# Attention's PSUM in two rings of banks, and bias products over the whole array

## The chip, the cores and the metric

The kernel runs on one NeuronCore of a Trainium2 chip. The metric is the time on the device in microseconds (us), of the one core, as the median of several executions. Engines are called by the names that the profile uses: PE is TensorE (matmuls), PEld its loading of stationary operands, DVE is VectorE, ACT is ScalarE, POOL is GpSimd, SP is SyncE, which here issues most DMA transfers.

## The reference

The input x has 32 sequences of 256 tokens with 128 features, so 8192 tokens. Four layers follow one another; each is

```python
x = x + attn(layernorm(x))
x = x + ffn(layernorm(x))
```

with these bodies:

- Layer 0: a projection to u, v and g of 256 features each; u goes through a depthwise convolution of three taps and silu, then through a diagonal state recurrence (64 states per feature); `y * sigmoid(g) + silu(v)` is projected back with a bias. The ffn has 16 experts of which each takes its best tokens, and a shared expert.
- Layer 1: linear attention with a gate and a causal mask (no softmax); the ffn has 8 experts of 512 hidden features with GELU, two per token, weighted, each `gelu(x @ w1 + b1) @ w2 + b2`, and a shared expert with biases.
- Layer 2: causal softmax attention with 16 heads of 8 features, low-rank projections; the ffn is a linear layer with a shared and six routed low-rank parts.
- Layer 3: a linear layer, a recurrence along the tokens, a second linear layer with bias `b_out`; the ffn is softmax attention over all keys of a sequence (16 heads of 8, biases), layernorms, and 8 experts (`relu(x @ w1 + b1) @ w2 + b2`, 256 hidden features), one per token.

For every softmax attention what has to come out is `softmax(q k^T / sqrt(8)) v`, then a product with `wo`.

## The kernel before, in words

Tokens lie as 64 tiles of 128 (partitions) by 128 features in the core's memory; four tiles make a block. The stages run one after another, and each opens its own pools of PSUM banks. By the time line: layer 0's mixer until about 330 us, its ffn until 750, layer 1 until 1310 and its experts until 1640, layer 2's attention from 1685 to 2240, layer 2's ffn and layer 3's mixer (function `middle`) until 2440, layer 3's attention until 3083, its experts until 3240, the rest until the end.

**Biases by matmul.** A bias row in f32 is split by `split` (L96) into three bf16 rows that add up to it. It is added to a PSUM tile by a matmul of these 3 rows with 3 rows of ones, as the first or last member of an accumulation. In layer 0's `project` (L757 to L774) the rows are 12 (`brow`, three for each of the four rows of `cwr`) and the other operand is `inside`, which says which tokens see which case. There are 128 of those, one after each six f32 matmuls over the whole 128 by 128 array; each such product is one quarter of a PSUM tile. The other places are layer 0's output (L872, 16 times), layer 1's values (L1463, 16), layer 1's output with the shared expert's bias (L1568, 16), `leave` in `middle` (L2280, 16) and the experts.

**Experts** (`Slots.experts`, L484). Tokens sorted by expert are gathered in groups of N = 2 tiles of 128. In `fetch` (L502) SP's DMA brings the group's rows `xs`, VectorE copies the expert's weights `w` (L515) and second bias `b2` (L517), PE transposes the rows (L522), VectorE copies them to `xT` (L524). `rise` (L527) makes the hidden features (L533) and ScalarE applies the activation (L539). `fall` (L544) makes the output: for each of two tiles the FC products (L549) and then the three-row bias (L553); VectorE multiplies by the token's weight (L555), and GpSimd sends both tiles to their places in DRAM (L479). The order for PE, ACT, DVE and SP is written by hand: rise(g), fetch(g+1), fall(g-1). Layer 1 has 72 groups with FC = 4, layer 3 has 40 with FC = 2.

**Attention** (L1603 to L1987), for layers 2 and 3. An item is one sequence; it takes four steps g = 0 to 3, each with four head pairs' worth of work (p, j). The order for PE, ACT and DVE is written by hand in `step` (L1921). For each of the four, two score products are made: `highs` (L1785) gives q by k, of which VectorE takes the row maximum in `maxima` (L1799, reduce at L1803); this runs LEAD = 7 steps ahead of the other, `weights` (L1842), which gives k by q with the maximum subtracted (it comes in through rows of q, the `row` below), and ScalarE makes the exponential `e` from it (L1857). In layer 2 `cover` (L1702) adds the mask by bf16 matmuls to both. `values` (L1860) of the step before multiplies `e` with the values, 16 small matmuls into the bank `o`; after g = 3 ScalarE copies `o` out.

Around these stand whole-array parts, once per item: `turn` (L1728) transposes the next input; `project` (L1739, matmul L1743) makes q and k, of which ScalarE copies the high part and VectorE (`lows`, L1754) the low part, and SP carries all to `qs` and `keys` through DRAM; `contents` (L1773) makes the values; `halve` (L1809) turns the maxima into a high and a low half on VectorE, `lower` (L1820) transposes them on PE, and its `place` has VectorE copy them to `row` and SP write them into `qs` (four DMAs); `heads` (L1883) transposes the output back on PE and VectorE divides by the sums (L1893, L1894); `back` (L1896) transposes again; `join` (L1904) is the product with `wo`, and its `add` has VectorE add it to x.

The work appended to the list `late` (`lows`, `place`, `add`) is emptied by `settle`, which runs after the first maximum of the next step. The step's order is: four times scores and maximum, with `settle` after the first; at g1 `heads`, at g2 `back`; `values`; at g0 `project` and `halve`; at g1 `lower` and `turn`, in one bank; at g3 `join` and `contents`, in one bank.

**PSUM.** [...] attention's pools are (L1714 to L1717) `ps` with 3 for `highs`, `pt` with 3 for `weights`, `pa` with 1 for `values`, and `pm` with 1, given out by `bank` (L1725), for all the whole-array parts. A tile from a pool waits until the tile that had the bank before is used up. `more` lets a caller place its own work at the end of a step: in layer 3 this is `gate` (L2412), which takes a tile from `bank` to transpose outputs and make the router's logits for the experts.

## Time and profile before

| | |
|---|---|
| median of 3 runs | 3316.81 us (3314.72 to 3318.75) |
| profiled execution, its own time | 3323.56 us |
| its span, first to last instruction | 3321.8 us |
| granted TensorE clock, mean | 0.89 |
| PE busy | 2661.6 us, 80% of the span |
| DVE busy | 1843.3 us, 55% |
| ACT busy | 1409.0 us, 42% |
| POOL busy | 844.5 us, 25% |
| largest group on DVE | L1803, the maxima: 1024 of 616 ns, 598.6 us |
| largest group on ACT | L1857, the exponentials: 1024 of 546 ns, 493.7 us |

The profiled execution is one run, recorded instruction by instruction. A group's line gives how often it ran, its busy time, the mean duration of one, and how long its engine stood idle just before its instructions, with what released them. A time line gives each instruction's start and duration. Matmuls overlap, so the distance between two starts is what one costs, not its duration. A step of attention is measured from the first L1849 of one step to that of the next.

### The profile page before, as it was taken

How to read it: one execution, taken by the hardware profiler on the slowest of the kernel's cores; microseconds unless marked ns; L12 is line 12 of the kernel's file. 1: busy time of each engine (PE TensorE's matmuls, PEld its weight loads, DVE VectorE, ACT ScalarE, POOL GpSimd, SP SyncE). 2: the span in 40 equal slices, each digit the busy share in tenths (PEclk: the TensorE clock that was granted, in tenths of full speed). 3: DMA queues.
4: the chain of work that ended last, by engine and by line, in shares of the span. 5: the costliest groups of instructions: out<-in, count | busy, mean ns of one | idle time of the engine just before them, and what ended most of it. 6: DMA issues, size and time to landing. Idle time of an engine off the chain costs nothing.

```text
span 3321.8 us, 59216 instructions
## 1 busy us (share of the span) xinstructions
PE 2661.6 (80%) x21597; PEld 1897.2 (57%) x21598; DVE 1843.3 (55%) x5368; ACT 1409.0 (42%) x2988; POOL 844.5 (25%) x1227
## 2 busy tenths in 40 slices
PE   5999778999795457999778998988988888786580
PEld 4765444446564335888656777757655555554460
DVE  6115445436874111333368877755788877774446
ACT  3323432223463222333425555557246655553123
POOL 0001444300015341444310010001501332323463
PEclk9899889999898778999869999997979988997795
DMA  2377455620002010122165444420054444440223
GB/s 67 110 247 238 177 233 228 232 73 6 11 1 88 26 35 15 60 62 61 55 180 152 131 138 141 131 64 1 8 147 119 116 115 115 122 115 13 83 80 107
DMA packets 263262, 340.80 MB, mean 103 GB/s; under 512 B 34598, under 2 KB 231062, under 8 KB 254780
## 3 DMA queue, kind: packets, MB, share of 16 engines
q1 hardware_dynamic: 231228, 237.01, 25.1%
q0 software_dynamic: 27584, 97.92, 7.7%
q8 instruction: 171, 2.80, 0.4%
q10 hardware_dynamic: 4160, 2.10, 0.2%
q14 instruction: 119, 0.97, 0.1%
HBM read 156.72 MB, written 177.83 MB: 101 GB/s over the span
## 4 chain that ended last, share of the span: by engine, by line
PE 36%; DVE 16%; issue 5%; another core or an unknown queue 5%; ACT 4%; DMA 3%; POOL 2%; SPq 1%; DVEq 0%; POOLq 0%; ACTq 0%
DVE top L1803 6%; PE hp L533 5%; PE o L549 5%; PE t L1849 4%; PE o L1870 4%; PE s L1791 2%; DMA q<-row 2%; PE o L1568 2%; POOL f_back L479 1%; ACT e L1857 1%; DVE st_x L241 1%; PE hp L1554 1%; PE m L1743 1%; PE m L1908 1%
## 5 line engine op out<-in xcount | busy, mean ns | idle before, releaser
L1803 DVE TENSOR_REDUCE top<-s 128x3 f32<-128x384 f32 (+1 forms) x1024 | 598.6, 616 | 212.9 <-PE s L1702 111.2
L1857 ACT ACTIVATE e<-t 128x384 f32<-128x384 f32 (+1 forms) x1024 | 493.7, 546 | 140.0 <-PE s L1702 76.6
L1849 PE MATMUL t<-q,k 64*128 64x256 f32 (+1 forms) x2048 | 422.9, 313 | 103.0 <-ACT e L1857 77.9
L1791 PE MATMUL s<-k,q 48*128 48x256 f32 (+1 forms) x2048 | 446.5, 333 | 12.7 <-DVE top L1803 10.1
L1849 PEld LDWEIGHTS t<-q,k 64*128 64x128 f32 x2048 | 303.4, 195 | 185.4 <-ACT e L1857 108.9
L1791 PEld LDWEIGHTS s<-k,q 48*128 48x128 f32 x2048 | 312.9, 201 | 27.4 <-DVE top L1803 20.0
L479 POOL DMA_INDIRECT f_back<-y,place x224 | 216.3, 965 | 313.1 <-DVE y L555 171.8
L539 ACT ACTIVATE h<-hp,w 128x256 f32<-128x256 f32 x368 | 154.6, 471 | 328.6 <-PE hp L533 287.2
L1870 PE MATMUL o<-e,val 128*32 128x256 f32 (+1 forms) x4096 | 270.2, 385 | 0.0
L549 PE MATMUL o<-w,h 128*128 128x128 f32 x1472 | 214.3, 284 | 0.0
L533 PE MATMUL hp<-xT,w 128*128 128x256 f32 x736 | 195.2, 405 | 21.2 <-DVE xT L524 15.6
L549 PEld LDWEIGHTS o<-w,h 128*128 128x128 f32 x1472 | 183.5, 193 | 7.7
L2039 POOL TENSOR_SCALAR xn<-x_sb,mean_x,r_x 128x128 f32<-128x128 f32 x64 | 53.0, 836 | 441.7 <-PE m L1732 387.2
L1870 PEld LDWEIGHTS o<-e,val 128*32 128x32 f32 x4096 | 112.0, 114 | 91.9 <-issue 38.8
L533 PEld LDWEIGHTS hp<-xT,w 128*128 128x128 f32 x736 | 134.2, 195 | 46.2 <-DVE xT L524 20.2
L1554 PE MATMUL hp<-xnT,shared 128*128 128x512 f32 x128 | 74.2, 709 | 103.4 <-ACT h L1558 93.2
L1702 PE MATMUL s<-hideq,pick 64*128 64x128 bf16 x1024 | 151.5, 231 | 0.0
L473 POOL DMA_INDIRECT f_rows<-row,slot x128 | 122.9, 960 | 110.3 <-ACT h L1558 66.9
L1702 PE MATMUL t<-hidek,pick 64*128 64x128 bf16 x1024 | 146.2, 226 | 0.0
L555 DVE TENSOR_TENSOR y<-o,xs 128x256 f32<-128x256 f32 x112 | 47.4, 424 | 164.4 <-PE o L553 149.2
L766 PE MATMUL up<-wc,hT 128*128 128x128 f32 x768 | 129.2, 309 | 0.0
L1574 DVE TENSOR_TENSOR x_sb<-x_sb,o 128x512 f32<-128x512 f32 x16 | 11.0, 687 | 209.9 <-remote 98.9
(515 smaller groups left out, 5392.8 us busy)
## 6 DMA issues: line engine op xcount, KB each, us to landing
f_rows<-blank POOLq DMA_DIRECT2D x176, 390.0 KB
tz<-kpad SPq DMA_DIRECT2D x64, 512.0 KB
d<-high SPq DMA_DIRECT2D x128, 256.0 KB
d<-low SPq DMA_DIRECT2D x128, 256.0 KB
q<-d SPq DMA_DIRECT2D x128, 256.0 KB
k<-d SPq DMA_DIRECT2D x128, 256.0 KB
xs<-f_rows SPq DMA_DIRECT2D x112, 130.0 KB
t<-f_back SPq DMA_DIRECT2D x24, 512.0 KB
```

Source lines behind the costliest of these rows:

```text
L473: i = self.K.nc.gpsimd.indirect_dma_start(self.rows, bass.IndirectOffsetOnAxis(ap=slot, axis=0), row, None)
L479: i = self.K.nc.gpsimd.indirect_dma_start(self.back, bass.IndirectOffsetOnAxis(ap=place, axis=0), row, None)
L533: nc.tensor.matmul(hp[:, i, :], w[:, (c + i) * P : (c + i + 1) * P], xT, start=True, stop=True,)
L539: nc.scalar.activation(h[:, c + i, :], hp[:, i, :], act, bias=w[:, b1 : b1 + 1])
L549: nc.tensor.matmul(o[:, i, :], h[:, c, i * P : (i + 1) * P], w[:, F + c * D : F + c * D + D], start=c == 0, stop=False,)
L766: nc.tensor.matmul(o, hT[:, 2 * blk + b, s : s + P], wc[:, j, cs], start=j == 0, stop=False)
L1702: nc.tensor.matmul(t.rearrange("p (n q) -> p n q", n=3)[:, 0:3:2, 64 * n : 64 * n + 64], pick[r, n, :], hide[name][r], start=False, stop=n ...
L1791: nc.tensor.matmul(s[:, lo:hi], q[r, p, h * P : (h + 1) * P], k[r, p, 0 : hi - lo], start=h == 0, stop=not causal and h == 1,)
L1803: nc.vector.tensor_reduce(tops[b][:, :, j, p], out_of["s"][:, 0:used].rearrange("q (h k) -> q h k", h=3 if causal else 2), axis=AX.X, op=A ...
L1849: nc.tensor.matmul(t[:, kh * SEQ : kh * SEQ + SEQ - skip], k[r, p, kh * P : (kh + 1) * P], q[r, p, skip:SEQ], start=kh == 0, stop=not caus ...
L1857: nc.scalar.activation(e, t, AF.Exp)
L1870: nc.tensor.matmul(o[32 * i : 32 * i + 32, skip:SEQ], val[b % RING][:, kh, 4 * m + i, 16 * s : 16 * s + 32], e[:, kh * SEQ : kh * SEQ + SE ...
```

## The change

It has two parts.

First, every operand of a bias matmul has 128 rows in place of 3 or 12. `split` returns a tile of 128 partitions that GpSimd has set to zero, with the rows written into its head; the ones, `inside` and the copies of `b2` have 128 partitions likewise. In `fall` one bias matmul, with `b2` repeated for both tiles, opens the accumulation of the whole bank, where two had closed it.

Second, attention's PSUM is given out as two rings. `pm` is gone. `ps`, whose tiles VectorE empties, has 4 banks in layer 2 (causal) and 3 in layer 3, and serves `highs`, `project`, `lower`, `heads`, `join` and `gate`. `pt`, whose tiles ScalarE empties, has 3 in layer 2 and 4 in layer 3 and serves `weights`, `turn`, `contents` and `back`. `values` comes ahead of all whole-array parts; `lower` stands right behind `halve` at g0 in place of g1, and the tile that it shared with `turn`, and that which `join` shared with `contents`, are two tiles each. The division in `heads` and VectorE's part of `gate` go on `late`; `more` is called ahead of the last `settle`.

```diff
@@ -95,9 +95,13 @@
         nc = self.nc
-        shape = list(t.shape)
-        hi, mid, out = (pool.tile(shape, BF16, name=f"{n}_{name}") for n in ("hi", "mid", "rows"))
+        n, *shape = t.shape
+        hi, mid = (pool.tile([n, *shape], BF16, name=f"{i}_{name}") for i in ("hi", "mid"))
+        full = pool.tile([P, *shape], BF16, name=f"rows_{name}")
+        nc.gpsimd.memset(full, 0.0)
+        out = full[0:n]
         nc.vector.tensor_copy(hi, t)
@@ -105,7 +109,7 @@
         nc.vector.scalar_tensor_tensor(out, hi, m[:, 0:1], out, ALU.mult, ALU.add)
-        return out
+        return full
@@ -513,8 +517,8 @@
                 nc.vector.tensor_copy(w, flat[:, bass.ds(at, REST)])
-                b2 = gp.tile([3, D], BF16, name="b2")
-                nc.vector.tensor_copy(b2, flat[0:3, REST:][:, bass.ds(at, D)])
+                b2 = gp.tile([P, D], BF16, name="b2")
+                nc.vector.tensor_copy(b2, flat[:, REST:][:, bass.ds(at, D)])
                 place = gp.tile([P, N], mybir.dt.uint32, name="place")
@@ -544,13 +548,16 @@
                 o = po.tile([P, N, D], F32, name="o")
+                nc.tensor.matmul(
+                    o, self.every, b2.unsqueeze(1).to_broadcast([P, N, D]), start=True, stop=False
+                )
                 for i in range(N):
                             o[:, i, :], h[:, c, i * P : (i + 1) * P],
-                            w[:, F + c * D : F + c * D + D], start=c == 0, stop=False,
+                            w[:, F + c * D : F + c * D + D], start=False,
+                            stop=i == N - 1 and c == FC - 1,
                         )
-                    nc.tensor.matmul(o[:, i, :], self.every[0:3, :], b2, start=False, stop=True)
                 y = gp.tile([P, N, D], F32, name="y")
@@ -723,13 +730,14 @@
         brow = K.split(sp, cwr, part, "brow")
-        inside = sp.tile([R, SEQ], BF16, name="inside")
-        nc.vector.tensor_copy(inside, valid)
+        inside = sp.tile([P, SEQ], BF16, name="inside")
+        nc.gpsimd.memset(inside, 0.0)
+        nc.vector.tensor_copy(inside[0:R], valid)
         half_g = sp.tile([P, 2], F32, name="half_g")
         obias = K.split(sp, out_b, K.parts(sp, 3), "obias")
-        ones3 = sp.tile([3, P], BF16, name="ones3")
-        nc.gpsimd.memset(ones3, 1.0)
+        every = sp.tile([P, P], BF16, name="every")
+        nc.gpsimd.memset(every, 1.0)
...
@@ -1286,11 +1294,10 @@
             K.second_biases(bp, b2, "f1_b2")
-            bv = sp.tile([3, D], BF16, name="bv")
+            bv = sp.tile([P, D], BF16, name="bv")
             nc.vector.tensor_copy(
             )
-        three = S.every[0:3, :]
@@ -1461,7 +1468,7 @@
                 nc.tensor.matmul(
-                    vp, three, bv.unsqueeze(1).to_broadcast([3, 4, D]), start=True, stop=False
+                    vp, S.every, bv.unsqueeze(1).to_broadcast([P, 4, D]), start=True, stop=False
                 )
...
@@ -1583,7 +1591,7 @@
                 assert not (active or ready or turned)
-                nc.scalar.copy(w_all[0:3, :, 2 * F + FC :], b2[:, 0:NE, :])
+                nc.scalar.copy(w_all[:, :, 2 * F + FC :], b2[:, 0:NE, :])
                 S.finish(rw, LONG, expert, start)
@@ -1711,10 +1719,10 @@
     dp = K.pool(es, tag + "d", 3, DRAM)
-    ps = K.pool(es, tag + "ps", 3, PSUM)
-    pt = K.pool(es, tag + "pt", 3, PSUM)
+    ps = K.pool(es, tag + "ps", 4 if causal else 3, PSUM)
+    pt = K.pool(es, tag + "pt", 3 if causal else 4, PSUM)
     pa = K.pool(es, tag + "pa", 1, PSUM)
-    pm = K.pool(es, tag + "pm", 1, PSUM)
     x_of, xT_of, tops, exps, out_of, on_of, oT_of = {}, {}, {}, {}, {}, {}, {}
@@ -1723,11 +1731,12 @@
     def bank():
-        return pm.tile([P, 512], F32, name="m")
-    def turn(b, t):
+        return ps.tile([P, 512], F32, name="s")
+    def turn(b):
         x = x_of.pop(b)
+        t = pt.tile([P, 512], F32, name="t")[:, 0:SEQ]
         for h in range(2):
@@ -1770,9 +1779,10 @@
-    def contents(b, t):
+    def contents(b):
         xT = xT_of.pop(b)
+        t = pt.tile([P, 512], F32, name="t")[:, 0:SEQ].rearrange("p (h d) -> p h d", h=2)
         for h in range(2):
@@ -1785,7 +1795,7 @@
         q, k = qs[b % RING], keys[b % RING]
-        s = out_of["s"] = ps.tile([P, 512], F32, name="s")
+        s = out_of["s"] = bank()
         r = slice(64 * j, 64 * j + TOP)
@@ -1817,10 +1827,10 @@
-    def lower(b, t):
+    def lower(b):
         cut = tops.pop(b)
-        t = t[0 : 2 * HEADS].rearrange("n (h q) -> n h q", h=2)
+        t = bank()[0 : 2 * HEADS, 0:SEQ].rearrange("n (h q) -> n h q", h=2)
         for h in range(2):
@@ -1843,7 +1853,7 @@
         r = slice(64 * j, 64 * j + 64)
-        t = pt.tile([P, used], F32, name="t")
+        t = pt.tile([P, 512], F32, name="t")[:, 0:used]
         for kh in range(2):
@@ -1888,22 +1898,29 @@
         t = t.rearrange("p h m (n c) -> p (h m n) c", c=16)
-        rec = wp.tile([P, 2 * HEADS], F32, name="rec")
-        on = on_of[b] = wp.tile([P, 2 * HEADS, HD], F32, name="on")
-        nc.vector.reciprocal(rec, t[:, :, ONE])
-        nc.vector.tensor_mul(on, t[:, :, 0:HD], rec.unsqueeze(2).to_broadcast([P, 2 * HEADS, HD]))
+        def divide():
+            rec = wp.tile([P, 2 * HEADS], F32, name="rec")
+            on = on_of[b] = wp.tile([P, 2 * HEADS, HD], F32, name="on")
+            nc.vector.reciprocal(rec, t[:, :, ONE])
+            nc.vector.tensor_mul(
+                on, t[:, :, 0:HD], rec.unsqueeze(2).to_broadcast([P, 2 * HEADS, HD])
+            )
+        late.append(divide)
         on = on_of.pop(b).rearrange("p (h n) c -> p h (n c)", h=2)
-        t = bank()[:, 0:SEQ]
+        t = pt.tile([P, 512], F32, name="t")[:, 0:SEQ]
         for h in range(2):
-    def join(b, t):
+    def join(b):
         oT = oT_of.pop(b)
+        t = bank()[:, 0:SEQ].rearrange("p (h d) -> p h d", h=2)
         for h in range(2):
@@ -1941,50 +1958,43 @@
                 beside()
-        if g == 1 and gone:
-            heads(before)
-        if g == 2 and gone:
-            back(before)
         if 0 <= t - 1 < total:
             halve(known)
+            lower(known)
         if g == 0 and then:
             x_of[ahead + 1] = rows(ahead + 1)
-        if g == 1:
-            known = a // TURNS - 1
-            if then or 0 <= known < NB:
-                m = bank()
-                if 0 <= known < NB:
-                    lower(known, m[:, SEQ:])
-                if then:
-                    turn(ahead + 1, m[:, 0:SEQ])
-        if g == 3 and (gone or fetch):
-            m = bank().rearrange("p (n h d) -> p n h d", n=2, h=2)
-            if gone:
-                join(before, m[:, 0])
-            if fetch:
-                contents(ahead, m[:, 1])
+        if g == 1 and gone:
+            heads(before)
+        if g == 1 and then:
+            turn(ahead + 1)
+        if g == 2 and gone:
+            back(before)
+        if g == 3 and gone:
+            join(before)
+        if g == 3 and fetch:
+            contents(ahead)
         beside()
+        more(t, bank, late)
         if t >= total:
             settle()
-        more(t, bank)
         for b in range(FIRST):
-            turn(b, bank()[:, 0:SEQ])
+            turn(b)
             project(b)
             settle()
-            contents(b, bank()[:, 0:SEQ].rearrange("p (h d) -> p h d", h=2))
+            contents(b)
         x_of[FIRST] = rows(FIRST)
         settle()
-        more(None, bank)
+        more(None, bank, late)
...
@@ -2318,7 +2328,7 @@
         y = row[:, :, 0:D]
-        b2 = sp.tile([3, NE, D], BF16, name="b2")
+        b2 = sp.tile([P, NE, D], BF16, name="b2")
         expert = sp.tile([1, S.groups], mybir.dt.int32, name="expert")
@@ -2409,7 +2419,7 @@
-            def gate(bank):
+            def gate(bank, late):
@@ -2431,19 +2441,23 @@
                     turned.append((new, yT))
-                if old:
-                    lo, at = old[0] // CHUNK * CHUNK, old[0] % CHUNK
-                    if at == 0:
-                        logits[lo] = lw.tile([P, CHUNK, NG + NE], F32, name="lge")
-                    nc.vector.tensor_add(
-                        logits[lo][:, at : at + 2, :], out,
-                        gate_b.unsqueeze(1).to_broadcast([P, 2, NG + NE]),
-                    )
-                    if at == CHUNK - 2:
-                        active.append((choose(lo), lo))
-                for g in count:
-                    hold[g[1]] = t[:, 384:512]
-                    go(g)
+                def then():
+                    if old:
+                        lo, at = old[0] // CHUNK * CHUNK, old[0] % CHUNK
+                        if at == 0:
+                            logits[lo] = lw.tile([P, CHUNK, NG + NE], F32, name="lge")
+                        nc.vector.tensor_add(
+                            logits[lo][:, at : at + 2, :], out,
+                            gate_b.unsqueeze(1).to_broadcast([P, 2, NG + NE]),
+                        )
+                        if at == CHUNK - 2:
+                            active.append((choose(lo), lo))
+                    for g in count:
+                        hold[g[1]] = t[:, 384:512]
+                        go(g)
+                late.append(then)
@@ -2539,16 +2553,18 @@
-            def more(t, bank):
+            def more(t, bank, late):
                     while active or pairs or turned:
-                        gate(bank)
+                        gate(bank, late)
+                        while late:
+                            late.pop(0)()
                         for g in list(active):
                 if t % TURNS == 2 or t >= NB * TURNS:
-                    gate(bank)
+                    gate(bank, late)
...
```

The hunks left out are the same edits as those at L1461 in layer 0's output, layer 1's output and `leave`, the three operands' new shapes there, and the new argument of `more` in layer 2.

## The prediction

> **What bounds the kernel now.** I read the page's first part (busy time by engine) and fourth part (the chain), then busy time by stage, then the instructions of one expert group and of one attention item.
>
> ```profile
> PE 2661.6 (80%) x21597; PEld 1897.2 (57%) x21598; DVE 1843.3 (55%) x5368; ACT 1409.0 (42%) x2988; POOL 844.5 (25%) x1227
> PE 36%; DVE 16%; issue 5%; another core or an unknown queue 5%; ACT 4%; DMA 3%; POOL 2%; SPq 1%; DVEq 0%; POOLq 0%; ACTq 0%
> ```
>
> TensorE sets the end where its order is not broken by a wait. By stage (us, then busy PE, weight loads, VectorE, ScalarE, GpSimd, clock, DMA share, GB/s), layer 1's experts, then layer 2's attention, then layer 3's:
>
> ```profile
> 1310.00:1640.00 330.00, 324.72 (x2016) 277.50 (x2016) 125.77 (x365) 122.14 (x290) 139.40 (x151) 0.98 0.20 58
> 1685.00:2240.00 555.00, 496.10 (x6837) 381.65 (x6836) 411.22 (x1254) 297.03 (x702) 48.22 (x77) 0.94 0.47 132
> 2441.00:3083.00 642.00, 507.42 (x4916) 330.36 (x4917) 471.15 (x1377) 370.78 (x793) 166.38 (x216) 0.88 0.36 103
> ```
>
> The experts are PE alone (98%). In layer 2 VectorE (74%) has slack, in layer 3 PE is idle for 21%. Who causes the idle time is in the groups of TensorE, first for 1745 to 2155 us (layer 2), then for 2500 to 2990 (layer 3); after the bar are busy us and mean ns, then idle us and releasers:
>
> ```profile
> L1849 PE MATMUL t<-q,k 64*128 64x256 f32 x404 | 150.2, 373 | 8.2 <-DMA q<-row 7.3 <-ACT val L1780 0.5
> L1825 PE MATMUL m<-ident,cut 128*32 128x128 f32 x50 | 9.7, 275 | 21.9 <-DVE on L1894 9.9 <-DVE v_x L268 6.3 <-DVE r_x L277 1.3
> ```
>
> ```profile
> L1849 PE MATMUL t<-q,k 64*128 64x256 f32 x816 | 161.8, 320 | 67.9 <-ACT e L1857 58.5 <-issue 9.1
> L1825 PE MATMUL m<-ident,cut 128*32 128x128 f32 x52 | 10.3, 280 | 18.1 <-DVE on L1894 6.7 <-DVE m L2475 3.5 <-DVE t_x L289 2.5
> ```
>
> The one `m` bank makes `lower` wait for `heads`' multiply (L1894), 22 and 18 us; in layer 3 the three `t` banks make weights wait for the exponential, 58 us.
>
> [...] the timeline of PE in one fall (start, duration) shows:
>
> ```profile
> 1434.31 1.06 PE L549 MATMUL o<-w,h 128*128 128x128 f32 x8
> 1435.30 0.22 PE L553 MATMUL o<-b,every 3*128 3x128 bf16 x1
> 1435.45 1.16 PE L549 MATMUL o<-w,h 128*128 128x128 f32 x8
> ```
>
> [...] one that waits for a bank holds all behind it, as the idle before L1825 shows. [...] the pools used 3+3+1+1 of them, so the four banks of a ring are found by giving up `m`.
>
> **The bias edits.** From the single instructions: pitch of L549's matmuls 0.112 us; previous matmul to bias 0.207 (+0.095); bias to next 0.154; that one's follower comes at 0.214 instead of 0.112 (+0.10). One three-row bias costs 0.095+0.154+0.10 = 0.35; a group has two, 0.70. A whole-array bf16 product is visible elsewhere:
>
> ```profile
> 1010.31 0.22 PE L398 MATMUL u<-taken,first 128*128 128x128 bf16 x1 [1.30 <-DVE lg L1349]
> 1010.37 0.22 PE L399 MATMUL u<-taken,every 128*128 128x128 bf16 x1
> 1010.42 0.55 PE L1509 MATMUL o<-v,a 128*128 128x129 f32 x3
> ```
>
> Pitch 0.055 for 128 columns, then f32 follows with some 0.055 extra and no drain. The new bias has 256 columns: 0.11+0.055 = 0.165, or 0.215 if the switch of type costs more. Saved per group 0.49 to 0.54. In layer 1 (72 groups, period 4.44, PE busy throughout) that is 35 to 39: **−37**. GpSimd's two sends (2.5 us) and ScalarE (1.9) stay under 3.9; gathered rows land 4.45 us after their issue with some 5.05 left to them, so they stay hidden.
>
> In layer 3 (40 groups) the period is set by those rows instead: two groups per some 6.5 us, which is place to y two groups later 1.53, 0.45, landing 4.5. A fall shorter by 0.5 shortens a pair by up to 0.5: 20 pairs, 0 to 10, taken **−9**.
>
> In layer 0's projection the 12-row bias follows every six matmuls, 128 times, at 0.352 each by the same three gaps (0.73 in cold stretches). With 128 columns the new one is 0.11 to 0.165: 0.19 to 0.24 saved, ×128 = 24 to 31 if PE sets all. The second half of it has PE busy 90 of 90 us, but DMA share 0.70, 0.74 at the shorter time; the first half waits in some blocks for VectorE's layernorm. I take **−20** (−10 to −28). 64 more (L872, L1463, L1568, leave) stand mostly in waits: **−4**. The new memsets (six in `split`, one for `inside`) are GpSimd's, in stages' openings beside loads: 0 to +2, taken 0. The wider copies of b2 have the same length per partition: 0. Sum: −37−9−20−4 = **−70** (−50 to −85).
>
> **The attention edits.** Per item (four steps g0 to g3) the steps start, by L1849, at these medians apart: layer 2: 3.68, 4.7, 2.98, 3.8 = typically 15.7, mean 16.07; layer 3: 3.81, 5.6, 3.84, 3.87 = 17.1. All my time inside a step is from its first score.
>
> Gains. [...] The wait before L1825 goes too (21.9 us over the window's 25 items, 0.88 each), and layer 3's wait for the exponential at g1 (58.5 us over 26 items, 2.3 each).
>
> Costs. Every whole-array tile that VectorE empties (project's by `lows`, lower's by the copy to `row`, heads' by `divide`, join's by add, all of them after the next step's first maximum) now sits in a ring with the scores. A score waits for the tile four back (three in layer 3), and everything behind it on PE waits too, the weights' products and so ScalarE's exponentials. VectorE, from DVE's timeline in layer 2 around g1:
>
> ```profile
> 1969.41 0.17 DVE L1812 TENSOR_TENSOR top<-top 128x16 f32<-128x16 f32 x1
> 1969.93 0.18 DVE L1818 TENSOR_TENSOR cut<-top,high 128x32 f32<-128x32 f32 x1
> 1970.26 0.56 DVE L1803 TENSOR_REDUCE top<-s 128x3 f32<-128x384 f32 x1
> 1970.73 0.75 DVE L1758 TENSOR_TENSOR low<-m,high 128x256 fp32r<-128x256 f32 x2
> 1971.39 1.48 DVE L1803 TENSOR_REDUCE top<-s 128x3 f32<-128x384 f32 x3
> ```
>
> The first maximum ends at 0.66+0.47 = 1.13 after the step's start, the two `lows` at about 1.88, `row` behind them at 2.2, `divide` (0.35+0.42 with gaps) at 1.98, add (0.41) at 1.58. Natural score starts in layer 2: 0, 0.38, 0.80, 1.28, phase 1.83.
>
> Layer 2, ring of four. g0: the fourth score waits for add (1.28 to 1.58: +0.30); `lower`, now behind project, waits for halve (0.7 us of VectorE after the last maximum): +0.3 to 0.5, and its own 0.22; 3.68 becomes 4.6 to 4.8. g1: the third score is four behind project's tile: waits for `lows` to 1.9 instead of 0.80: stall 1.13, score phase 1.83+1.13, values 0.79, heads and turn 0.80: 4.55 against 4.7. g2: fourth score waits for `divide`, 1.28 to 1.98: 2.98+0.71 = 3.70. g3: 3.71 against 3.8. Sum 16.6 to 16.7 against 15.7 to 16.07: +0.6 to +1.0, times 32 items = 19 to 32, **+25**. `place` is issued earlier, but its four row transfers stand on SP behind d<-high, d<-low, q<-d and k<-d, 11.4 to 12 us from g1 to landing, so it brings the rows no sooner; the wait for q<-row (7.3 us) stays.
>
> Layer 3, ring of three, natural scores at 0, 0.34, 0.58, 0.82, end 1.04. g0: third waits for add (1.63), scores end 2.12; `lower` waits for halve, 4.4 to 4.7: 4.92 against 3.81. g1: second waits for `lows` (2.07), third for `row` (2.4), end 2.82: 4.83 against 5.6, where the exponential's wait had been. g2: third waits for `divide` (2.02), end 2.46: 4.60 against 3.84. g3: third waits for the gate's add (1.33): 4.1 against 3.87. Sum 18.45 against 17.1: +1.35, times 32 = 43; a stretch of items 20 to 26 loses time to GpSimd's sends whatever PE does, so **+36** (0 to +47).
>
> **Sum.** −70+25+36 = −9: the profile's own 3323.6 us becomes 3314.6. The median is 6.8 less, 3316.8−9 = **3308**.
>
> **The rivals.**
> - Waits only move, because VectorE has 26% spare and its order lets the ring run ahead: attention comes out even. For it: the 22, 18 and 58 us of idle that go. Against: the first maximum stands ahead of `lows`, `divide` and add in VectorE's order. −70: 3247.
> - Slower: project's tile in VectorE's ring. In g1 the score that needs its bank waits for `lows`, and the stall is passed to the exponentials, values and the next step's maxima. The price has to pass 70 us, 1.1 us per item over 64 items, to decide; at 1.5 (my 1.35 of layer 3 in both layers, and a little for later rows) it is +95: 3342. [...] Against: layer 2 has a fourth bank.
> - Attention gains: a fourth `t` bank ends the 58 us of waits, and L1825's 40 go[...] minus small new waits: −40 beside −70: 3207.
> - The bias edit doesn't do what it says: the gaps are of bf16 beside f32, not of three rows. Then only having one product in place of two helps: 72×0.35 = 25, little more elsewhere, about −28; with +61: 3350. Against: the L398 to L1509 pitch.
>
> **How the numbers follow.** My forecast, net −30 to +12: 0.37 (range 3287 to 3329). Even attention 0.25; slower 0.25; attention gains 0.06; bias ineffective 0.07. The 8-in-10 range leaves out attention's gain, and the upper ends of the last two: 3238 (even attention, bias at −79) to 3360. A measurement of this kernel tells 0.2%, 6.6 us. Faster: even and gaining (0.31) and half of mine (0.19) = 0.50; same: a third of mine, 0.12; slower: a sixth of mine with the two slower cases, 0.38.
>
> **What would show it.** Right: an expert group of 3.9 us in layer 1 with one bias of 0.165 and no 0.207 gap; in g1 an idle before L1791 put down to DVE `low` (L1758 or L1760), in g2 to `on`, in g0 L1825 released by `cut`; in layer 3 no wait of L1849 for `e`; items of 16.6 and 18.4 us. Wrong: if L1791's idle stays under 0.3 us per item, attention is even or gains; if the group stays above 4.2, the row count was not the drain; if experts of layer 1 show PE waiting for xs, the rows were not hidden.

## The result, and the profile after

The changed kernel takes **3294.29 us** (median of 5, 3284.55 to 3301.19) against 3316.81: ratio 0.9927, 95% interval 0.9904 to 0.9949. The forecast was 3308, 9 us less than before; it became 22.5 less. The profiled execution took 3286.0 us with a span of 3284.3, so it is one of the shorter of the five, 37.5 below that of before.

Where the time went, by stage, from the first and last instructions of the stages in the two profiled executions (us):

| stage | before | after | difference | in the forecast |
|---|---|---|---|---|
| layer 0's mixer, from the first projection | 327.0 | 295.6 | −31.4 | −20 and part of −4 |
| layer 1's shared expert | 286.0 | 275.6 | −10.4 | part of −4 |
| layer 1's experts | 332.3 | 288.0 | −44.3 | −37 |
| layer 2's attention | 545.6 | 579.3 | **+33.7** | +25 |
| layer 3's attention | 641.3 | 670.0 | **+28.7** | +36 |
| layer 3's experts | 181.4 | 174.6 | −6.8 | −9 |
| all else | 1008.2 | 1001.2 | −7.0 | 0 |

The bias part gave more than forecast and attention lost what was forecast, +62 against +61. But in layer 2 most of the loss is not made of the waits that the forecast lists. First the parts that went as written: TensorE's timeline in layer 1's experts (start, duration) after the change:

```profile
1292.31 1.24 PE L537 MATMUL hp<-xT,w 128*128 128x256 f32 x5
1293.39 0.38 PE L526 MATMUL t<-ident,xs 128*128 128x128 f32 x2
1293.61 0.27 PE L551 MATMUL o<-b,every 128*128 128x256 bf16 x1
1293.72 1.95 PE L556 MATMUL o<-w,h 128*128 128x128 f32 x16
1295.50 0.38 PE L537 MATMUL hp<-xT,w 128*128 128x256 f32 x1
```

One bias product, 0.11 us to the next start (it lasts 0.27; the two overlap) and no gap ahead of it, where the forecast had 0.165 to 0.215. The sixteen matmuls of `fall` (two are recorded for each f32 product) run through. The group takes 3.85 us in place of 4.44, 0.59 less. In layer 0's projection it is 0.06 in place of 0.154:

```profile
171.25 0.94 PE L774 MATMUL up<-wc,hT 128*128 128x128 f32 x6
172.02 0.22 PE L777 MATMUL up<-rows_brow,inside 128*128 128x128 bf16 x1
172.08 0.33 PE L774 MATMUL up<-wc,hT 128*128 128x128 f32 x1
```

Then attention. Busy time, clock and DMA of its two stages after (columns as in the prediction):

```profile
1598.00:2177.00 579.00, 528.43 (x6826) 398.29 (x6827) 405.04 (x1226) 302.13 (x697) 48.08 (x67) 0.89 0.44 124
2358.00:3028.00 670.00, 554.45 (x4951) 364.70 (x4951) 477.74 (x1354) 390.47 (x792) 160.56 (x211) 0.88 0.36 103
```

The same products as before (6826 for 6837 recorded) keep TensorE busy 528 us in layer 2 in place of 496, and the granted clock is 0.89 in place of 0.94. Idle time did not grow, as the groups of TensorE from 1655 to 2095 us (layer 2) show:

```profile
L1859 PE MATMUL t<-q,k 64*128 64x256 f32 x411 | 154.9, 379 | 7.1 <-ACT val L1790 5.5 <-issue 0.8 <-DMA q<-row 0.6
L1835 PE MATMUL s<-ident,cut 128*32 128x128 f32 x52 | 10.3, 280 | 22.6 <-DVE cut L1828 10.7 <-DVE dif_x L261 4.7 <-DVE r_x L299 4.4
```

`lower` waits as long as before (22.6 us for 21.9), now for `halve`; the wait for the rows is gone (0.6 for 7.3). From 2450 to 2960 us (layer 3):

```profile
L1859 PE MATMUL t<-q,k 64*128 64x256 f32 x793 | 184.1, 326 | 0.0
L1801 PE MATMUL s<-k,q 48*128 48x256 f32 x793 | 172.8, 335 | 74.3 <-DVE top L1813 67.1 <-DVE low L1769 3.8 <-issue 1.0
```

The weights' wait for the exponential (67.9 us of idle before) is zero; the scores stand idle 74.3 us in its place, for VectorE. Before, from 2500 to 2990 us, it was 0.6:

```profile
L1791 PE MATMUL s<-k,q 48*128 48x256 f32 x816 | 160.9, 320 | 0.6 <-DVE top L1803 0.4 <-issue 0.2
```

That is the trade that the two rings make in layer 3.

What took the time in layer 2 shows when each item (0 to 31) is taken alone. Items 19 to 22 (the item's window, then the columns as above):

```profile
1953.21:1969.30 16.09, 14.72 (x215) 11.34 (x215) 10.92 (x28) 9.83 (x23) 1.57 (x2) 1.00 0.46 135
1969.30:1984.69 15.39, 14.67 (x215) 11.35 (x216) 10.92 (x28) 9.08 (x21) 1.57 (x2) 1.00 0.49 141
1984.69:2001.85 17.16, 16.17 (x215) 12.15 (x214) 12.75 (x44) 9.46 (x22) 1.57 (x2) 0.90 0.44 125
2001.85:2019.01 17.16, 16.16 (x215) 12.11 (x215) 11.25 (x31) 9.46 (x22) 1.57 (x2) 0.90 0.45 128
```

The same 215 matmuls take 14.7 us of TensorE at clock 1.00 and 16.2 at 0.90. Inside the third of these items, at the end of g0, in slices of 0.68 us:

```profile
1987.66:1988.34 0.68, 0.68 (x4) 0.35 (x2) 0.68 (x2) 0.37 (x1) 0.00 (x0) 1.00 0.00 0
1988.34:1989.02 0.68, 0.10 (x1) 0.00 (x0) 0.58 (x5) 0.55 (x2) 0.00 (x0) 1.00 0.00 0
1989.02:1989.70 0.68, 0.39 (x4) 0.21 (x4) 0.39 (x4) 0.10 (x1) 0.00 (x0) 1.00 0.00 0
```

And in two stretches of 3.41 us, the second of which is the one at half clock:

```profile
1988.58:1992.00 3.42, 2.57 (x34) 2.05 (x34) 2.48 (x11) 1.87 (x5) 0.00 (x0) 1.00 0.46 153
1992.00:1995.41 3.41, 3.41 (x29) 2.08 (x27) 1.61 (x7) 0.78 (x3) 0.17 (x1) 0.50 0.72 204
```

TensorE is idle for 0.87 us ahead of `lower` at the end of g0; 2.7 us after that, and after the score stall at the start of g1, the clock is halved for 3.4 us, and g1 takes 5.45 us in place of 4.08. Of items 8 to 28 of layer 2, 9 stand below a clock of 0.95; before the change it was one. In the 3.42 us ahead of this drop TensorE counts as busy for 2.57.

In all 13 traces every change of the clock lies on one grid of 3.413 us, to within 4 ns (1.4 in that of the result). So it matters where an item falls on that grid. An item that is hit takes some 17 us, about five periods (17.07), so the next one falls on nearly the same place and is hit too: items 21 to 28 follow one another.

### The profile page after: what moved, and what is told of

It reads as the page before. It is cut to its first block, busy times and chain, and to the rows that moved or that the text cites. A ratio compares the mean times of both kernels' runs of the same rounds, so it can differ in the third digit from the quotient of the medians.

```text
span 3284.3 us, 59072 instructions
## 1 busy us (share of the span) xinstructions
PE 2612.5 (80%) x21486; PEld 1904.8 (58%) x21486; DVE 1844.3 (56%) x5368; ACT 1434.8 (44%) x2988; POOL 851.7 (26%) x1234
## 4 chain that ended last, share of the span: by engine, by line
PE 36%; DVE 18%; another core or an unknown queue 5%; issue 5%; POOL 3%; ACT 2%; DMA 1%; SPq 1%; DVEq 0%; ACTq 0%; POOLq 0%
DVE top L1813 7%; PE o L1880 6%; PE t L1859 4%; PE hp L537 4%; PE o L556 4%; PE s L1801 3%; POOL f_back L483 2%; DVE st_x L245 2%; PE o L1576 1%; PE s L1899 1%; PE s L1925 1%; PE hp L1561 1%; PE s L1710 1%; PE t L1710 1%
## 5 line engine op out<-in xcount | busy, mean ns | idle before, releaser
L1867 ACT ACTIVATE e<-t 128x384 f32<-128x384 f32 (+1 forms) x1024 | 511.9, 543 | 188.6 <-PE s L1710 93.9
L1801 PE MATMUL s<-k,q 48*128 48x256 f32 (+1 forms) x2048 | 466.7, 343 | 110.4 <-DVE top L1813 81.8
L1859 PE MATMUL t<-q,k 64*128 64x256 f32 (+1 forms) x2048 | 465.2, 321 | 15.4 <-ACT val L1790 5.5
L1859 PEld LDWEIGHTS t<-q,k 64*128 64x128 f32 x2048 | 325.5, 200 | 65.2 <-issue 33.4
L1880 PE MATMUL o<-e,val 128*32 128x256 f32 (+1 forms) x4096 | 284.6, 401 | 0.0
L537 PE MATMUL hp<-xT,w 128*128 128x256 f32 x736 | 186.2, 393 | 30.5 <-DVE xT L528 17.7
L556 PE MATMUL o<-w,h 128*128 128x128 f32 x1472 | 185.2, 278 | 0.0
L556 PEld LDWEIGHTS o<-w,h 128*128 128x128 f32 x1472 | 175.9, 194 | 1.6
L1561 PE MATMUL hp<-xnT,shared 128*128 128x512 f32 x128 | 74.3, 713 | 105.4 <-ACT h L1565 101.2
L336 POOL DMA_DIRECT2D f_rows<-blank x176 | 98.3, 558 | 54.5 <-POOL blank L332 51.5
```

Source lines behind the costliest of these rows:

```text
L537: nc.tensor.matmul(hp[:, i, :], w[:, (c + i) * P : (c + i + 1) * P], xT, start=True, stop=True,)
L556: nc.tensor.matmul(o[:, i, :], h[:, c, i * P : (i + 1) * P], w[:, F + c * D : F + c * D + D], start=False, stop=i == N - 1 and c == FC - 1,)
L1561: nc.tensor.matmul(hp, shared[:, c * P : (c + 1) * P], xnT[:, blk, :], start=True, stop=True)
L1801: nc.tensor.matmul(s[:, lo:hi], q[r, p, h * P : (h + 1) * P], k[r, p, 0 : hi - lo], start=h == 0, stop=not causal and h == 1,)
L1859: nc.tensor.matmul(t[:, kh * SEQ : kh * SEQ + SEQ - skip], k[r, p, kh * P : (kh + 1) * P], q[r, p, skip:SEQ], start=kh == 0, stop=not caus ...
L1867: nc.scalar.activation(e, t, AF.Exp)
```

## The experiments

The kernels were timed in five sittings: in two of them (the result; e5 to e8) the kernel before took 3317 to 3319 us, in the other three (e1 to e4; e9 and e10; e11) 3146 to 3156; these are called the first and the second place. So ratios to before in the same sitting are compared, and stages only within one place or where they agree. Items are counted from 8 to 28 of each layer, "low" below a clock of 0.95.

**The two parts alone.** e1 takes the bias edits without those of attention and `gate`, e2 the others.

```diff
 e1:
-        three = sp.tile([3, P], BF16, name="three")
+        every = sp.tile([P, P], BF16, name="every")
...
 e2:
-    pm = K.pool(es, tag + "pm", 1, PSUM)
+    ps = K.pool(es, tag + "ps", 4 if causal else 3, PSUM)
+    pt = K.pool(es, tag + "pt", 3 if causal else 4, PSUM)
...
```

> The kernel before with the bias edits alone; attention, its banks and gate as before. My theory (the two parts add up, and the bias part gives what the stages outside attention gained, about -98 us): 3219 us, layer 2's attention 545 us from its first score to its last join and layer 3's 654, as before. Rival (the bias part is worth my -70 and the rest of the gain came with the attention part, by the clock or by shifted transfers): 3247. Rival (attention's loss comes from the bias edits too): attention's stages 579 and 683, time 3290.

> The kernel before with the attention edits alone (two rings, order, late parts), biases with 3 and 12 rows. My theory: +62 us, 3379; layer 2's attention 579 us with steps g0 4.65 in undisturbed items, layer 3's 683. Rival (waits only move): 3317, stages 545 and 654. Rival (attention gains and something else lost it): 3277.

Measured: e1 3060.99 us, **0.9732** (0.9706 to 0.9758), layer 2's attention 543.7 us as before. e2 3207.83 us, **1.0219** (1.0179 to 1.0258). The product is 0.9945, and the changed kernel has 0.9927: the parts add up, attention is a loss on its own, and the rival of moving waits only falls. Scaled to the first place that is −89 and +73 us.

By stage, layer 2's attention takes 543.7 us in e1 and 555.8 in e2, layer 3's 596.2 and 629.5. The 579 that was expected for layer 2 in e2 is missed: only 1 of its 21 items is low, against 9 in the changed kernel's trace with the same attention. So the new order costs +12 us in layer 2 with hardly a drop of the clock, and +33 in layer 3, where 14 of 21 items are low and 6 in e1. The traced execution of e2 was the shortest of its four (3191.0 us to 3227.9).

**Rows or number of products.** e3 keeps one opening product per group but gives it three rows.

```diff
-    o, self.every, b2.unsqueeze(1).to_broadcast([P, N, D]), start=True, stop=False
+    o, self.every[0:3, :], b2[0:3].unsqueeze(1).to_broadcast([3, N, D]),
+    start=True, stop=False,
```

> As the bias edits alone, but the experts' one opening bias product has 3 rows in place of 128 (256 columns as there). It tells the drain from the number of products. If the drain of the short product is the cost: a group of layer 1's experts takes 0.24 to 0.35 us more than the 3.85 with 128 rows, about 4.1 to 4.2, and the experts' stage of layer 1 some 17 to 25 us more. If it was only that two products became one: 3.85, no difference.

Measured: one time, 3085.68 us. From the first to the last product of `fall` in layer 1 it takes 293.8 us against 273.1 of e1, +20.7, or 0.29 per group (in nine other kernels with 128 rows it is 272.8 to 273.2). TensorE's timeline, to be read against the one above (its line L557 is L556 there):

```profile
1199.19 0.38 PE L526 MATMUL t<-ident,xs 128*128 128x128 f32 x2
1199.51 0.28 PE L551 MATMUL o<-b,every 3*128 3x256 bf16 x1
1199.71 2.05 PE L557 MATMUL o<-w,h 128*128 128x128 f32 x16
```

The gap ahead grows from 0.22 to 0.32 after the pair of transposes, the one behind from 0.11 to 0.20, and the sixteen matmuls take 2.05 in place of 1.95. So the number of rows is what costs, in the same three places as before, and they add up to the 0.29. This extra time around a short product is what the prediction and the expectation call its drain; what TensorE does in it the traces don't show. From before (315.9 us) to e1 this stretch gained 42.8 us: 20.7 are the rows of the product that is left, and the other 22 the product that went.

**`lower` back at g1.** e4 is the changed kernel with one call moved.

```diff
             halve(known)
-            lower(known)
...
+        if g == 1 and 0 <= a // TURNS - 1 < NB:
+            lower(a // TURNS - 1)
         if g == 1 and gone:
             heads(before)
```

> The changed kernel with the transposes of the maxima (lower) put back to g1, behind values, in a tile of the VectorE ring of their own; all else as changed. My theory: the 0.9 us in which TensorE waits for halve at the end of g0 and the wait for lows at the start of g1 together make the clock drop to half in many items (0.90 over an item), worth 1.4 us each time. With lower moved g0 is 3.7 to 4.0 in place of 4.65, g1 4.3 to 4.6 and at full clock, so layer 2's attention falls from 579 us to 550, layer 3's from 683 to 660, time about 3245. Rival (the wait for lows alone makes the drop, or lower's wait goes elsewhere): items at 0.90 remain, stages within 8 us of 579 and 683, time 3280 to 3294.

Measured: 3068.94 us, **0.976** (0.974 to 0.978), 1.7% less than the changed kernel. In the median g0 is 3.68 in layer 2 and 4.14 in layer 3, g1 3.68 and 4.51. In layer 3 low items fall from 14 of 21 (e2, the changed attention in the same place) to 4, and the stage from 629.5 us to 591.0. In layer 2 another wait comes, which neither theory named; TensorE's group from 1540 to 2000 us:

```profile
L1859 PE MATMUL t<-q,k 64*128 64x256 f32 x448 | 166.8, 374 | 25.1 <-DMA q<-row 23.7 <-ACT val L1790 1.4
L1835 PE MATMUL s<-ident,cut 128*32 128x128 f32 x56 | 11.5, 288 | 0.0
```

With `lower` a step later the rows are late: 23.7 us of waiting at the end of g3, and 7 low items of 21 where e2 had one. So layer 2 takes 550.0 us, only 6 less than in e2, and the theory's 550 has another composition than it said.

**Filling the wait.** If idle time drops the clock, useless work in it must raise it. e6 puts redundant products ahead of `lower` into the bank that its transposes overwrite; e9 puts half as many.

```diff
+        t = bank()
+        if xT is not None:
+            for _ in range(4 if causal else 2):      # e9: 2, 1
+                nc.tensor.matmul(t[:, 0:SEQ], wq, xT, start=True, stop=True)
-        t = bank()[0 : 2 * HEADS, 0:SEQ].rearrange("n (h q) -> n h q", h=2)
+        t = t[0 : 2 * HEADS, 0:SEQ].rearrange("n (h q) -> n h q", h=2)
...
-            lower(known)
+            lower(known, xT_of[ahead] if g == 0 and fetch else None)
```

> The changed kernel itself, for the times and the trace on the chip of the next runs. If the two parts add up (0.9732 and 1.0219 of before were measured for them alone): 0.9945. Items of attention at 0.90 of the clock, with g1 some 1.4 us longer, in about a third of layer 2's items and half of layer 3's.

> The changed kernel with redundant matmuls put into the wait for halve at the end of g0: four products of 256 columns (two in layer 3) of q's projection into the bank that lower's transposes then overwrite, 0.22 us each; nothing else moves and no wait ends earlier. My theory (TensorE's idle at the end of g0, 1.0 us in layer 2, drops the clock together with the wait in g1): the items at 0.90 all but vanish, layer 2's attention is 10 to 30 us shorter than that of the changed kernel on this chip, though TensorE has more to do. Rival (the lower clock comes from the load, or from the wait in g1 alone): as many items at 0.90 or more, stages the same or up to 10 us longer.

> As the filled wait, with half of the redundant products: two of 256 columns in layer 2, one in layer 3. Measured with four and two: each is 0.43 us (two passes of 0.22), so 1.74 us overran the wait and g0 went from 4.65 to 5.62. Now 0.87 and 0.43. My theory: g0 stays within 0.1 of 4.65 to 4.93 (layer 3: 4.97 to 5.1), items of layer 2 below a clock of 0.95 after the first eight stay at one or two, so layer 2's attention is 545 to 560 us, layer 3's under the changed kernel's; time 0.985 to 0.990 of before against 0.9935 of the changed kernel. Rival (the lower clock needs the wait to be overfilled): as many drops as the changed kernel, 0.993.

Measured, low items of 21 in layer 2 and layer 3: changed kernel 9 and 12, again (e5) 3 and 14, its attention alone (e2) 1 and 14; filled (e6) 1 and 7; half filled (e9) 1 and 5. e5: 0.9935 (0.991 to 0.9961). e6: 0.9959 (0.9938 to 0.9981), no gain, since each product is 0.43 us, recorded as two matmuls, and four overran the wait: g0 went to 5.62, layer 2 to 573.1 us from 566.2 of e5, while layer 3, hardly overfilled, fell from 680.5 to 666.5. e9: g0 4.86, and **0.9856** (0.9818 to 0.9895), in the second place, where e1 and e2 make 0.9945 for the changed kernel (0.9927 and 0.9935 were measured for it in the first): less, though it does more work. Of its stages only layer 3's is shorter, 609.1 us for 629.5 of e2; layer 2's is 568.3, over the 545 to 560 expected and over e2's 555.8. In layer 3, items 9 to 11 of e5, then of e6, whose redundant products stand among its 162 matmuls:

```profile
2553.38:2573.04 19.66, 16.86 (x157) 11.13 (x156) 13.71 (x36) 12.48 (x25) 1.41 (x2) 0.91 0.38 110
2573.04:2591.14 18.10, 15.31 (x157) 10.25 (x156) 13.75 (x36) 12.48 (x25) 1.42 (x2) 1.00 0.40 120
2591.14:2610.83 19.69, 16.89 (x158) 11.03 (x157) 14.20 (x33) 12.47 (x25) 12.22 (x18) 0.91 0.39 109
```

```profile
2549.03:2567.38 18.35, 16.00 (x162) 11.07 (x162) 13.71 (x36) 12.55 (x25) 1.41 (x2) 1.00 0.41 118
2567.38:2587.31 19.93, 17.57 (x162) 11.93 (x162) 13.74 (x36) 12.55 (x25) 1.41 (x2) 0.91 0.38 109
2587.31:2605.66 18.35, 15.99 (x161) 11.07 (x161) 13.74 (x33) 12.55 (x25) 10.71 (x15) 1.00 0.40 117
```

How many items are hit differs between executions with the same attention (9, 3 and 1 in layer 2); this goes with the spread of the changed kernel's times, 3284.6 us at a mean clock of 0.887 to 3301.2 at 0.878, which for before was 4 us in that sitting. So the bare counts prove little; the grid of the clock's changes settles it. Take how long after an edge of the grid an item's g1 starts, and call the item hit if the clock is half from the next edge on. (The bounds are read from these traces.)

| g1 starts this long after an edge | changed attention (result, e2, e5) | with redundant products (e6, e9) |
|---|---|---|
| layer 2, 0.77 to 1.43 us | 13 of 16 hit | 0 of 6 |
| layer 2, elsewhere | 0 of 47 | 0 of 36 |
| layer 3, 0 to 0.85 us | 19 of 21 | 8 of 8 |
| layer 3, 0.85 to 1.7 us | 16 of 17 | 0 of 11 |
| layer 3, elsewhere | 0 of 25 | 0 of 23 |

So the idle time at the end of g0 is a cause of the drops, and not the load: filled, it makes no drop in the places where nearly every item had one. It is not the only cause. The items of layer 3 that stay hit are those whose g1 starts less than 0.85 us after an edge. The wait lies from 0.9 to 0.3 us before g1, so the 3.413 us from that edge hold a part of it or nothing, and the two stalls inside g1 (0.70 and 0.16 us) whole. And the counts differ because executions put different numbers of items into the bad place, in layer 2 9, 4 and 3. What decides over a drop is not shown: in item 9 of layer 2 of the changed kernel the 3.413 us between two edges in which TensorE counts as busy for 0.66 of the time passed without one, while those of item 21, with 0.75, did not.

**Towards a better order.** e7 keeps the old banks and puts `heads` behind `values`; e8 mends the rings; e10 fills the wait with `heads` itself; e11 takes e10 in layer 2 and e7 in layer 3.

```diff
 e7, on e1:
-        t = bank().rearrange("p (h m c) -> p h m c", h=2, m=2)
+        t = ps.tile([P, 512], F32, name="s").rearrange("p (h m c) -> p h m c", h=2, m=2)
...
 e8, on e4 (and lower behind heads at g1):
-        late.append(divide)
+        divide()
-                    nc.sync.dma_start(
+                    (nc.gpsimd if causal else nc.sync).dma_start(
...
 e10, on e8 (heads and lower at g1 only if not causal):
             halve(known)
+        if causal and g == 0 and gone:
+            heads(before)
+        if causal and g == 0 and 0 <= known < NB:
+            lower(known)
```

> The bias edits with attention as before, except that heads stands behind values at g1 and takes its bank from the scores' ring (three banks), its division at once; lower and turn keep the bank m, which then no longer waits for the division. My theory: in layer 2 g1 falls from 4.67 to 3.8 (no wait of L1825's transposes[...]), g0, g2, g3 stay at 3.68, 2.98, 3.7 and more; 32 items give 20 to 28 us; in layer 3 g1 keeps the wait for the exponential and loses 0.5: 16 us. About 40 us under the bias edits alone, 0.960 of before. Rival (the rows land later or the division is late for g2): under 10 us gained.

> The changed kernel with lower at g1 behind heads, the division at once in place of late, and the four transfers of row issued by GpSimd in layer 2 (SP in layer 3). My theory: against lower at g1 alone, layer 2's g2 falls from 3.35 to 3.0 and g3 from 4.6 to 3.7 to 4.0, as the rows no longer stand on SP behind k<-d: 550 to 510 us; layer 3's g2 from 4.73 to 3.9: 591 to 565; 0.955 of before. Rival (the rows are late by their own transfer, not by SP's queue): g3 stays at 4.6 and layer 2 at 540.

> The mended ring, but in layer 2 heads and lower both stand at g0 behind project: heads' transposes fill the wait for halve with work that has to be done, and the rows are ready a step earlier; rows by GpSimd in layer 2 as there. Layer 3 as in the mended ring. My theory: layer 2's steps 4.6, 3.5, 2.98, 3.7 and no wait for q<-row, 14.8 per item: 515 us against 544; time 0.958 to 0.961 of before against 0.9673. Rival (the division, now at g0's end, delays the first maximum of g1, or the rows' transfers are slow by themselves): 535 to 550, 0.966 to 0.970.

> The bias edits, layer 2's attention as in heads in the wait (two rings, heads and lower at g0), layer 3's as in heads behind (three score banks, three for the weights, the bank m, heads behind values). My theory (the stages stand for themselves): layer 2's items 14.9 to 15.2 at mean 15.2, layer 3's 16.2 to 16.4 in place of 16.8; about 17 us under heads in the wait, 0.960 of before. Rival (layer 3's gain is lost to the stretches in which GpSimd holds the items): 0.965, as heads in the wait.

| kernel | ratio to before | layer 2, mean item | low | layer 3, mean item of 13 | low of 21 |
|---|---|---|---|---|---|
| e1 | 0.9732 (0.9706 to 0.9758) | 15.66 | 0 | 17.20 | 6 |
| e7 | 0.9704 (0.9684 to 0.9724) | 16.43 | 9 | 16.33 | 7 |
| e8 | 0.9673 (0.9652 to 0.9694) | 15.73 | 4 | 16.87 | 4 |
| e10 | 0.9653 (0.9598 to 0.9707) | 15.20 | 1 | 17.00 | 2 |
| e11 | 0.9637 (0.9612 to 0.9661) | 15.26 | 2 | 16.53 | 5 |

(The 13 items leave out those in and beside the stretches in which GpSimd sends rows to DRAM and VectorE stands still. In item 18 of the result GpSimd has eight sends from 2734.0 to 2744.0 us, and VectorE is idle for 7.64 us until 2746.1, which the profile puts to "remote"; the item takes 29.4 us.) In e7 layer 2's g1 fell to 3.75 as expected, and g3 rose from 4.0 to 5.0: the rows became late, 30.8 us of waiting, and layer 2 lost more than it had gained; the whole gained 0.3% over e1 in place of the 1.3% expected, so its rival was right. In e8 GpSimd issues the last of the rows 11.1 us into the item (12.9 in e4), but they are ready no sooner: 24.8 us of waiting remain, and 0.9673 in place of 0.955, so its rival was right for layer 2. e10 makes the rows a step earlier and has work in the wait; TensorE's groups from 1600 to 2060 us:

```profile
L1859 PE MATMUL t<-q,k 64*128 64x256 f32 x436 | 161.8, 378 | 2.9 <-DMA q<-row 1.6 <-ACT e L1867 1.1
L1835 PE MATMUL s<-ident,cut 128*32 128x128 f32 x52 | 9.8, 270 | 11.3 <-DVE cut L1828 11.3
```

Its items are 14.87 to 15.15 us nearly throughout, and layer 2's stage 536.1 us, where e2 has 555.8 in the same place. Items 0, 3 and 6 still stand at clocks of 0.63 to 0.71, and the stage is not the 515 expected: 536.1 us and 0.9653 are numbers that its rival had named, though the wait for the rows went (1.6 us) as the theory said. e11 can't be told from e10: its 13 items in layer 3 are shorter, but the whole stage is not (573.9 us and 573.3), so its rival was right. Both beat the kernel before and the changed one, and e11 and e8 are also clear of e1.

## Why the prediction was right, and where its steps were not

The sum was right in kind: the biases gain more than attention loses. That attention's +61 met the measured +62 so nearly is in part luck, since layer 2's share came about in another way.

- **Bias sum, −70.** Right in kind, too small: −84.5 us of 3145.5 in e1. The terms that were mis-sized are the new product (0.11 us measured, 0.165 to 0.215 taken; no switch of type shows) and layer 0: −31 against −20. There the second half's blocks fell from 5.53 to 4.70 us, the full 0.21 per bias, with DMA share at 0.84; and in the first half (33 to 135 us before, 33 to 120 after) the clock rose from 0.83 to 0.92, which the working left out. Layer 3's experts gave 7, forecast 9. The wider copies of `b2`, taken as free, take 230 ns in place of 222; the seven new memsets take 3.2 us of GpSimd, and what they add to the time is not measured.
- **Attention, +61.** Measured +62 in the two traces; e2 gives +62 of 3145.5 by its median, +45 in its traced execution. Of layer 3's steps 4.92, 4.83, 4.60, 4.10, undisturbed items show 4.97 to 5.07, 4.65, 4.41, 4.07: 18.1 to 18.2 against 17.0 to 17.1. That mechanism was right, with its place (the scores wait for VectorE, the exponential's wait is gone) and nearly its size. Its order was not: in g1 the second score starts at 1.32, behind the first maximum (1.26), where it was to wait for `lows` (2.05), and 67.1 of the 74.3 us are put down to maxima. A waiting score did hold the weights behind it: in item 18 of layer 3 both start at 2746.83 us, after 4.68 us of idle.
- **"A score waits for the tile four back" failed in layer 2.** g1 is 4.08 where 4.55 was forecast, g2 2.98 where it was 3.70. In g1 of item 20 the scores start at 0, 0.38, 1.28 and 1.94; the first maximum ends at 1.23, `lows` at 1.89. So the third score waits for the first maximum and the fourth for `lows`: the bank that is released first is given out next, and `settle` runs after the first maximum. `divide` holds no score in g2 at all. Items at full clock thus take 16.1 us in the median and 15.4 at the shortest, 0.4 over before's 15.65 and 15.03, not 16.6. The starts fit this order of release; no run changed it alone. The prediction's own sign for an attention that comes out even, under 0.3 us of idle per item at the scores, came in layer 2 (4.5 us in 26 items), and attention lost all the same.
- **Layer 2's sum.** Step by step the forecast's own medians differ by +1.5 us (4.7 for 3.68, 4.55 for 4.7, 3.70 for 2.98, 3.71 for 3.8), which is 48 us in 32 items. It held their sum, 16.6, against whole items of 15.7 to 16.07, which are longer than the sum of their medians, and so had +25.
- **"Idle" was priced at its own length.** That is the step that is missing. The waits were summed, and the clock was taken as given. The waits alone made +12 us of layer 2 (e1 and e2); the other 22 of the +34 go with the drops of the clock, each of which makes g1 1.4 us longer. e6 and e9 show that the idle time is a cause of them (0 of 17 items hit where 29 of 33 had been).
- **"It brings the rows no sooner" held, "the wait stays" did not.** SP issued the first of the four at 7.5 us of the item in place of 10.5, ahead of k<-d, but the last at 12.6 as before (medians). The wait fell from 7.3 to 0.6 us as the item became longer: its end, where the rows are used, came 3.8 us behind the last issue in place of 3.1. But in e2, where that is 3.7, 5.5 us of waiting remain, so how much of it goes is not settled. e4, e7 and e8 show the other side: with `lower` at g1 and the item shorter, the rows cost 24 to 31 us.
- **`lower`'s wait.** As forecast it is now for `cut` (10.7 of the 22.6 us; the rest is put down to other work of VectorE), and it did not go.
- **The rivals.** Even attention is excluded by e2, and attention that gains too. The slower kernel needed over 70 us from attention, and +62 came. Ineffective bias falls with e1 and e3.

## What to carry to other kernels

A product with few rows between whole-array ones cost its neighbours too (e3: 0.10 us ahead of it, 0.09 behind it and 0.10 in the matmuls that follow): pad it, and merge what can be merged. Before a tile that is emptied late is put in a ring with tiles emptied at once, write down in which order banks are released, not only how many there are; and price an idle stretch of TensorE also by what it does to the clock of the next microseconds (0.87 us of it went with 1.4 us more of g1), so that work that has to be done goes into the wait. A transfer that an early step feeds has its slack there: moving that step back, or shortening the item around it, can turn a hidden transfer into the longest wait (the rows in layer 2: 0.6 us of waiting in the changed kernel, 23.7 in e4).

## What the runs showed of the hardware that was not expected

- A wait of 0.87 us and short stalls behind it, between two edges of the grid, 3.413 us in which TensorE still counts as busy for three quarters, are followed by half the clock for 3.4 us. The grid runs through the whole execution in each trace, so one and the same item is hit or spared by where it falls on it (13 of 16 hit in one stretch of layer 2's, 0 of 47 elsewhere), and the spread of one kernel's times (17 us here) goes with how many are hit. e9, with redundant products, takes 0.9856 of before; for the same kernel without them e1 and e2 make 0.9945.
- With padding the clock was higher as well: over the first 576 matmuls recorded for `project` in layer 0 it is 0.87 and 0.88 in the two kernels with 12 rows (before, e2), and 0.89 to 0.94 in the eleven with 128.
- The same code takes 286 and 276 to 280 us in layer 1's shared expert in one place and 163 to 167 in the other, with idle time that the profile puts to "remote" and to the engines' issue; what it waits for there is not shown.
